# Storing a band of attention weights with shifted rows, and padding the next layer's weights earlier, in a two-layer kernel

## The chip, the core and the metric

The kernel runs on one core of a Trainium2 chip. Such a core has five engines with a queue of instructions each: TensorE (PE in the profile; its weight loads are shown apart as PEld), VectorE (DVE), ScalarE (ACT), GpSimd (POOL) and SyncE (SP), which here only issues transfers. Each queue runs in its order, and an instruction whose operands are not ready holds up everything behind it in its queue. Transfers between the core's memory and HBM are carried out by 16 DMA engines. The metric is the device time of one launch in microseconds (us); lower is better.

## The reference, cut to what matters

The input x has 4 rows (B) of 512 positions (T) with 128 channels (C). Two layers follow one another; each normalises x and adds an attention and a mixture of experts to it.

```python
# layer 0, attention: 16 heads, every position t sees the 64 positions that end with it
strain  = disp_win - disp[:, :, :, None, :]                  # 16 numbers per pair (t, d)
logits  = gelu(strain @ W_strain + rel_emb @ W_pos) @ W_bond \
          - 10 * sigmoid(gelu(strain @ W_dmg + b_dmg) @ W_dmg_out + b_dmg_out)
weights = softmax(where(in_range, logits, -inf))             # over the 64 distances
out     = einsum('bntd,bntde->bnte', weights, val_win)       # then @ W_cproj
# layer 0, experts: 16 gated experts, the best 4 of each position weigh in
# layer 1, attention: 16 heads of 8 channels over all 512 positions
q, k, v = split(x @ w_qkv)
out     = softmax(q k^T / sqrt(128)) v                       # then @ w_out
# layer 1, experts: 8 experts relu(x W1) W2, the best 2 of each position weigh in
```

So in layer 0 the attention weights of a row form a band: for every head and position, 64 numbers, one per distance.

## The kernel before

**Order of the program.** The kernel is written as generators, one for each job, which `weave` runs in turn by given step counts. The text's order gives each instruction its rank. A planner then places the instructions on the five queues: of those whose operands and buffers its estimated times say are ready, the one of the highest rank goes first. It also gives out the buffers of each pool and sets the semaphore waits. Every DMA takes one of a fixed set of completion semaphores, in turn. Where the planner's order was not wanted, explicit dependencies were added (`add_manual_dep`), as for the products of `hidden` (L378), which follow the products of layer 1's attention once these have begun.

**The rows' slots.** The loop at L719 goes over the rows b = 0 to 3. A slot weaves, for its own row, `band_logits(b)` and `gated_experts(b)`; for the row before, `band_values(b - 1)` and then the beginning of layer 1's `relu_experts(b - 1)`; for the row before that, the rest of `relu_experts`; and for the next row `prepare(b + 1)`. Each slot has two halves, two calls of `weave`. Layer 1's attention for all rows (`full_attention`) begins after the loop, woven with `band_values(3)` and what is left of the experts.

**band_logits (L543).** The 128 partitions hold 16 heads by 8 distances d8: partition 64 dq + 4 h + dd is head h at distance d8 = 4 dq + dd, and an outer loop `do` steps the distance by 8. For each `do` and each of the two kinds of activation, VectorE writes four differences into tiles z (L560, 128 x up to 2,048 numbers), ScalarE applies Gelu (L562, L566), and TensorE reduces them into a bank (L574). The pool of the z tiles has four buffers. At the end the maxima are exchanged over transposes (L603 to L612), and for each of two halves of `do` VectorE subtracts the maximum into a tile e, which is taken from the same four buffers (L616), ScalarE takes the exponential (L620), and one DMA stores e to a scratch tensor `by_t` in HBM (L621): 128 rows of 8 KB.

**band_values (L304).** For each of the row's four tiles of 128 positions (st), eight DMAs (L312) load a tile f from `by_t`: 128 partitions by 8 by 128 numbers. A weight belongs to the query position; to stand by the position it looks at, the row of distance d8 = 4 dq + dd is read from d8 places further on, which is why every (dq, dd) has its own DMA of 16 rows. `by_t` has rows of 8 T = 4,096 numbers (L291), and a last row of zeros for reads past the end (L476). TensorE transposes f (L321), ScalarE copies the result to g (L322), and g goes to a second scratch tensor `by_s` (L327), from which the tile wb is read back with a slanted pattern (L338) and multiplied with the values (L348, L352). f has two buffers.

**The weights of layer 1's attention.** After the loop and after layer 0's pools are closed, at L747 to L758: w_qkv is loaded (L748), a tile wqk is zeroed by GpSimd (L753), and VectorE copies the query and the key part into it, each head's 8 columns padded to 32 (L755). `queries` (L810) and `keys` (L819) multiply with wqk, `values` (L798) with w_qkv. Scores are products at L920, their maxima are taken by VectorE at L936.

**prepare (L492)** normalises row b and makes the projections from it, in three tiles of a pool `prep`: xn, xnT and sq, of 2 KB a partition each. The pool belongs to layer 0 and is closed with it; after `prepare(3)`, in row 2's slot, it is not used.

Of the kernel before, what the change touches and what calls it, by code (L numbers as in the profile page):

```python
# [22 lines left out]
FP = mybir.dt.float32  # L23
# [5 lines left out]
P = 128  # L29
# [3 lines left out]
H = 16  # L33
# [58 lines left out]
def weave(*tracks):  # L92
    for _ in woven(*tracks):
        pass
# [3 lines left out]
def two_layers(ctx: ExitStack, tc: tile.TileContext, w: dict, consts: bass.AP, out: bass.AP):  # L98
# [185 lines left out]

    chain = ctx.enter_context(tc.tile_pool(name="chain", bufs=2))
    wp = ctx.enter_context(tc.tile_pool(name="wp", bufs=2))
    xT = keep.tile([C, B * T], FP, name="xT")

    ROW = 8 * T  # L291
    by_t = dram.tile([P + 1, ROW], FP, name="by_t")
    by_s = dram.tile([T, H * BW], FP, name="by_s")

    wT_all = dram.tile([E0, P, 3 * P], FP, name="wT_all")
# [8 lines left out]
    def band_values(b, valn):  # L304

        o = chain.tile([P, TPB, C], FP, tag="o", name="o", bufs=1)
        for st in range(TPB):
            f = wp.tile([P, 8, P], FP, tag="f", name="f")
            for dq in range(2):
                for dd in range(4):  # L310
                    at = by_t.offset + (dq * 64 + dd) * ROW + st * P + 4 * dq + dd
                    nc.sync.dma_start(  # L312
                        out=f[dq * 64 + dd:(dq + 1) * 64:4],
                        in_=bass.AP(by_t.tensor, at, [[4 * ROW, H], [T + 8, 8], [1, P]]),
                    )
            yield
            g = wp.tile([P, H, WIN], FP, tag="g", name="g", bufs=1)
            for half in range(2):
                pt = bank()
                for i in range(4):  # L320
                    nc.tensor.transpose(pt[:, i * P:(i + 1) * P], f[:, 4 * half + i, :], ident)  # L321
                nc.scalar.copy(  # L322
                    g[:, :, 32 * half:32 * half + 32].rearrange("p h (q d) -> p q h d", d=4),
                    pt.rearrange("p (q h d) -> p q h d", h=H, d=4),
                )
            rows = by_s[st * P:(st + 1) * P, :]
            nc.sync.dma_start(out=rows.rearrange("s (h c) -> s h c", h=H)[:, :, 0:WIN], in_=g)  # L327
            v = va[st % 2]
            nc.scalar.copy(v[:, :, 0:8], valn[:, st, :].rearrange("p (h e) -> p h e", e=8))
            yield  # L330
            acc = bank()
            for half in range(2):
                wb = wp.tile([P, 8, BW], FP, tag="w", name="wb")
                for own in (True, False)[:1 + (st > 0)]:
                    s = st if own else st - 1
                    n = P if own else BW - P
                    at = by_s.offset + s * P * H * BW + half * 8 * BW + (0 if own else P)
                    nc.sync.dma_start(  # L338
                        out=wb[:, :, 0:P] if own else wb[:, :, P:BW],
                        in_=bass.AP(by_s.tensor, at, [[H * BW - 1, P], [BW, 8], [1, n]]),  # L340
                    )
                for g4 in range(2 * half, 2 * half + 2):
                    for own in (True, False)[:1 + (st > 0)]:
                        for hh in range(4):
                            h = g4 * 4 + hh
                            at = acc[hh * 32:hh * 32 + 32, g4 * P:(g4 + 1) * P]
                            if own:
                                nc.tensor.matmul(  # L348
                                    at, va[st % 2][:, h, :], wb[:, h % 8, 0:P], start=True, stop=(st == 0)
                                )  # L350
                            else:
                                nc.tensor.matmul(  # L352
                                    at[:, 0:BW - P], va[(st - 1) % 2][:, h, :], wb[:, h % 8, P:BW],
                                    start=False, stop=True,
                                )
            avs = chain.tile([P, 4, P], FP, tag="avs", name="avs", bufs=1)
            nc.scalar.copy(avs.rearrange("p g t -> p (g t)"), acc)
            pt = transposed(avs)
            pt3 = pt.rearrange("p (h e) -> p h e", h=H)
            rd = small.tile([P, H, 1], FP, tag="rd0", name="rd")  # L360
            nc.vector.reciprocal(rd, pt3[:, :, 8:9])
            nc.vector.tensor_tensor(
                o[:, st, :].rearrange("p (h e) -> p h e", h=H), pt3[:, :, 0:8],
                rd.to_broadcast([P, H, 8]), ALU.mult,
            )
            yield
# [89 lines left out]


    with ExitStack() as l0:
        prep = l0.enter_context(tc.tile_pool(name="prep", bufs=1))
        hold = l0.enter_context(tc.tile_pool(name="hold0", bufs=2))  # L460
        zp = l0.enter_context(tc.tile_pool(name="zp", bufs=4))
        lp = l0.enter_context(tc.tile_pool(name="lp", bufs=1))
# [10 lines left out]
        for st in range(TPB):  # L473
            nc.gpsimd.dma_start(out=by_s[st * P:(st + 1) * P, 0:2048], in_=zero)
            nc.gpsimd.dma_start(out=by_s[st * P:(st + 1) * P, 2048:H * BW], in_=zero[:, 0:H * BW - 2048])
        nc.gpsimd.dma_start(out=by_t[P:P + 1, 0:128], in_=zero[0:1, 0:128])  # L476


# [64 lines left out]
        def band_logits(b):  # L543
# [70 lines left out]
            for half in range(2):  # L614
# [3 lines left out]
                    pt[:, None, :].to_broadcast([P, 4, T]), ALU.subtract,  # L618
                )
                nc.scalar.activation(e, e, AF.Exp)  # L620
                nc.sync.dma_start(  # L621
                    out=by_t[0:P, 4 * half * T:(4 * half + 4) * T], in_=e.rearrange("p a t -> p (a t)")
                )
            yield

        def expert_weights(e, b):
# [20 lines left out]
        def gated_experts(b):  # L647
# [40 lines left out]
            finish(*late)  # L688
            add_rows(b, ya)

        preparation = prepare(0)
        for _ in range(2):
            next(preparation)
# [25 lines left out]
        for b in range(B):  # L719
            logits_b, gated_b = band_logits(b), gated_experts(b)  # L720
            if not b:
                weave((logits_b, 6), (preparation, 4))
            first = [(logits_b, 30 if b else 24), (gated_b, 7)]
            second = [(logits_b, 37), (gated_b, 10)]
            if b:
# [18 lines left out]
    def abank():  # L744
        return ps_a.tile([P, T], FP, tag="a", name="abank")

    w_qkv = one.tile([C, 3 * C], FP, name="w_qkv")  # L747
    nc.sync.dma_start(out=w_qkv, in_=w["L1_attn_w_qkv"])  # L748
    w_out = one.tile([C, C], FP, name="w_out")
    nc.sync.dma_start(out=w_out, in_=w["L1_attn_w_out"])  # L750

    wqk = one.tile([C, 2, 4, 4, 32], FP, name="wqk")
    nc.gpsimd.memset(wqk, 0.0)  # L753
    for s in range(2):
        nc.vector.tensor_copy(  # L755
            wqk[:, s, :, :, 0:8].rearrange("c g h e -> c (g h) e"),
            w_qkv[:, s * C:(s + 1) * C].rearrange("c (h e) -> c h e", e=8),
        )  # L758

    vaug = [one.tile([P, TPB, H, 32], FP, name=f"vaug{i}") for i in range(2)]  # L760
    nmax = [one.tile([P, TPB, 4, 32], FP, name=f"nmax{i}") for i in range(2)]
# [7 lines left out]
    def full_attention():  # L769
# [37 lines left out]
        def queries(n):  # L807
            b, g = groups[n]
            pq = abank()
            nc.tensor.matmul(  # L810
                pq, wqk[:, 0, g].rearrange("c h e -> c (h e)"), xT[:, b * T:(b + 1) * T], start=True, stop=True
            )
            q[n] = work.tile([P, T], FP, tag="q", name="q")
            nc.scalar.copy(q[n], pq)

        def keys(n):
            b, g = groups[n]
            pk = abank()
            nc.tensor.matmul(  # L819
                pk, wqk[:, 1, g].rearrange("c h e -> c (h e)"), xT[:, b * T:(b + 1) * T], start=True, stop=True  # L820
            )
            k[n] = work.tile([P, T], FP, tag="k", name="k", bufs=3)
            nc.scalar.activation(k[n], pk, AF.Identity, bias=c_("ones8"))
# [165 lines left out]
```

## Time and profile before

| | us |
|---|---|
| median of three runs | 1378.02 (1374.11 to 1379.18) |
| the profiled execution, its own time | 1381.3 |
| its span, first to last instruction | 1379.5 |
| TensorE busy | 1174.3 (85%) |
| VectorE busy | 1012.4 (73%) |
| ScalarE busy | 1018.5 (74%) |
| GpSimd busy | 96.9 (7%) |
| layer 0 | 0 to about 930 |
| the four pairs of stores by_t<-e issued from | 236.0, 470.8, 705.1, 929.6 |
| first product of layer 1's attention (L810) | 943.0 |

A busy time is the sum over the span; an engine at 85% on average can be full in one stage and half idle in another. The profile's chain of waits goes back from the last instruction, at each step to what released it. Its shares by engine are TensorE 59%, ScalarE 17%, VectorE 13%, DMA 6%. The time of a DMA is given from its issue on a queue to its landing. A queue's issue is an instruction of its own with its own length.

| DMA | times | KB each | us to landing | issue on SP, ns (least/median/most) |
|---|---|---|---|---|
| f<-by_t (L312) | 128 | 64 | 3.1 | 537/599/1790 |
| by_t<-e (L621) | 8 | 1,024 | | 319/320/320 |
| wb<-by_s (L338), the larger form | 32 | 512 | 4.1 | 360/527/2791, both forms |
| by_s<-g (L327) | 16 | 512 | 4.2 | 553/559/570 |
| wT<-wT_all (L630) | 48 | 192 | 3.0 | 319/320/1648 |
| r<-route (L672, L432) | 96 | 256 | 3.5 | 319/327/1532 (L672) |

### The profile page before, as it was taken

Reading aid. Unit: us, or ns where it says so; the run is one execution under the profiler, and the core shown is the slowest. Engines: PE = TensorE matmul, PEld = TensorE weight load, DVE = VectorE, ACT = ScalarE, POOL = GpSimd, SP = SyncE. Lnnn points to the kernel's source line nnn. Section 1 sums busy time; section 2 is a strip of 40 time slices with the busy share of each in tenths; the row PEclk is TensorE's granted clock in tenths of the full one; section 3 lists DMA queues with packets and bytes.
Section 4 is the critical chain, followed back from the end, with each engine's and each line's share of the span. In section 5 each row is a group of like instructions: output and inputs, shape, how many; then the busy total and the mean of one; then the engine's idle time right before and its main releaser. Section 6 shows DMA issues by size and latency. Waiting matters only on the chain.

```text
span 1379.5 us, 17426 instructions
## 1 busy us (share of the span) xinstructions
PE 1174.3 (85%) x6763; PEld 450.2 (33%) x6763; DVE 1012.4 (73%) x1085; ACT 1018.5 (74%) x1160; POOL 96.9 (7%) x68
## 2 busy tenths in 40 slices
PE   5676976678889789889989988887999899999997
PEld 2122323123433323353333334232333332333322
DVE  4999998999866999987799998843444434444451
ACT  4899997999968899988889988862454435545554
POOL 2000000000000002200002320012000000000000
PEclk9799998899879999999999999999999989999999
DMA  7121213446212445622244751235133200011100
GB/s 268 44 74 52 76 52 103 100 118 153 62 41 75 150 102 145 170 64 64 73 153 110 180 131 48 67 96 166 49 88 77 69 9 24 24 38 39 31 16 8
DMA packets 168524, 117.61 MB, mean 85 GB/s; under 512 B 66621, under 2 KB 149274, under 8 KB 166906
## 3 DMA queue, kind: packets, MB, share of 16 engines
q1 hardware_dynamic: 166970, 109.77, 29.3%
q0 software_dynamic: 1184, 6.29, 1.2%
q8 instruction: 54, 0.88, 0.3%
q10 hardware_dynamic: 288, 0.43, 0.1%
q14 instruction: 28, 0.23, 0.1%
HBM read 89.00 MB, written 27.46 MB: 84 GB/s over the span
## 4 chain that ended last, share of the span: by engine, by line
PE 59%; ACT 17%; DVE 13%; DMA 6%; issue 5%; SPq 0%; DVEq 0%; ACTq 0%
PE score L920 11%; PE lbank L574 10%; PE bank L381 8%; PE bank L442 7%; ACT z L566 6%; DVE z L560 5%; PE accbank L838 4%; ACT z L562 3%; PE gbank L674 3%; PE accbank L663 3%; DMA wb<-by_s 3%; PE gbank L681 2%; DMA wT<-wT_all 2%; DVE nmax L936 2%; PE abank L810 1%
## 5 line engine op out<-in xcount | busy, mean ns | idle before, releaser
L560 DVE TENSOR_TENSOR z<-proj 128x2044 f32<-128x2044 f32 (+31 forms) x256 | 554.1, 2189 | 29.0 <-PE lbank L574 12.6
L574 PE MATMUL lbank<-z,place 128*32 128x504 f32 (+18 forms) x2048 | 288.9, 639 | 110.1 <-ACT z L566 68.8
L936 DVE TENSOR_REDUCE nmax<-score 128x2 f32<-128x1024 f32 x128 | 156.3, 1225 | 182.3 <-PE score L920 180.1
L566 ACT ACTIVATE z<-z,posb 128x1024 f32<-128x1024 f32 (+31 forms) x256 | 267.3, 1097 | 10.2 <-DVE z L560 8.2
L942 ACT ACTIVATE ex<-score 128x1024 f32<-128x1024 f32 x128 | 130.3, 1023 | 159.7 <-PE score L920 159.7
L562 ACT ACTIVATE z<-z,brep 128x2048 f32<-128x2048 f32 (+31 forms) x128 | 241.4, 1906 | 5.3 <-DVE z L560 4.9
L920 PE MATMUL score<-k,q 32*128 32x512 f32 x512 | 152.2, 655 | 13.9 <-DVE nmax L936 11.7
L447 POOL TENSOR_TENSOR total<-total,part 128x512 f32<-128x512 f32 x32 | 82.6, 2580 | 1038.3 <-DVE part L446 1038.3
L920 PE MATMUL score<-qa,k 32*128 32x512 f32 x512 | 139.7, 648 | 2.1 <-ACT ex L942 2.1
L381 PE MATMUL bank<-xT,ew 128*128 128x512 f32 x256 | 136.2, 626 | 1.6 <-ACT h L389 0.8
L442 PE MATMUL bank<-h,ew 128*128 128x512 f32 x256 | 133.1, 619 | 4.7 <-issue 4.7
L389 ACT ACTIVATE h<-bank,cols 128x512 f32<-128x512 f32 x144 | 97.1, 684 | 45.3 <-PE bank L381 44.6
L574 PEld LDWEIGHTS lbank<-z,place 128*32 128x32 f32 x2048 | 43.0, 112 | 264.2 <-ACT z L566 143.9
L663 PEld LDWEIGHTS accbank<-wT,lin 128*128 128x128 f32 x512 | 72.2, 204 | 60.4 <-issue 34.6
L663 PE MATMUL accbank<-wT,lin 128*128 128x128 f32 x512 | 82.1, 297 | 10.1 <-DVE lin L661 10.1
L674 PE MATMUL gbank<-tT,wT 128*128 128x512 f32 x128 | 72.2, 647 | 17.4 <-DMA wT<-wT_all 16.5
L838 PE MATMUL accbank<-ex,vaug 128*32 128x512 f32 x512 | 70.8, 619 | 0.2 <-ACT ex L942 0.2
L681 PE MATMUL gbank<-tT,wT 128*128 128x512 f32 x128 | 70.6, 635 | 0.0
L920 PEld LDWEIGHTS score<-k,q 32*128 32x128 f32 x512 | 41.2, 187 | 89.0 <-ACT ex L942 44.1
L442 PEld LDWEIGHTS bank<-h,ew 128*128 128x128 f32 x256 | 44.2, 193 | 74.4 <-issue 71.0
L381 PEld LDWEIGHTS bank<-xT,ew 128*128 128x128 f32 x256 | 41.9, 192 | 72.8 <-issue 43.6
L659 DVE SCALAR_TENSOR_TENSOR lin<-lin,r 128x512 f32<-128x512 f32 x64 | 44.5, 695 | 28.6 <-ACT lin L683 28.3
(188 smaller groups left out, 1193.7 us busy)
## 6 DMA issues: line engine op xcount, KB each, us to landing
r<-route SPq DMA_DIRECT2D x96, 256.0 KB, 3.5
ew<-in_L_ffn_W SPq DMA_DIRECT2D x64, 256.0 KB, 3.4
wb<-by_s SPq DMA_DIRECT2D x32, 512.0 KB, 4.1
wT<-wT_all SPq DMA_DIRECT2D x48, 192.0 KB, 3.0
by_t<-e SPq DMA_DIRECT2D x8, 1024.0 KB
f<-by_t SPq DMA_DIRECT2D x128, 64.0 KB, 3.1
by_s<-g SPq DMA_DIRECT2D x16, 512.0 KB, 4.2
wb<-by_s SPq DMA_DIRECT2D x24, 256.0 KB, 3.6
```

Of the source, the lines that this page charges most:

```text
L381: mm = nc.tensor.matmul(ph, wt[:, c * P:(c + 1) * P], xT[:, b * T:(b + 1) * T], start=True, stop=True)
L442: nc.tensor.matmul(py, old[1][:, c, :], old[0][c], start=(c == 0), stop=(c == 3))
L560: nc.vector.tensor_tensor(z[:, :, :, 0:n], seen, own, ALU.subtract)
L562: nc.scalar.activation(z[:, :, :, 0:n], z[:, :, :, 0:n], AF.Gelu, bias=b_dmg)
L566: last = nc.scalar.activation(z[:, dq, :, 0:n], z[:, dq, :, 0:n], AF.Gelu, bias=posb[:, j:j + 1])
L574: mm = nc.tensor.matmul(ps[q:q + 32, t0:T], place[:, kind, 3 - dd:35 - dd], z[:, dq, hg, 0:n], start=(dd == 0), stop=(dd == 3),)
L663: nc.tensor.matmul(ya[:, i * P:(i + 1) * P], lin[:, i * P:(i + 1) * P], wT[:, 2, :], start=False, stop=(e == E0 - 1 and i == TPB - 1),)
L674: nc.tensor.matmul(pg, wT[:, 0, :], tT, start=True, stop=True)
L838: mm = nc.tensor.matmul(av[n][r:r + 32, :], vaug[b % 2][:, i, g * 4 + h, :], ex[n, i][:, h, :], start=(i == 0), stop=(i == TPB - 1),)
L920: mm = nc.tensor.matmul(ps[:, h - two, :], own[r, i * P:(i + 1) * P], seen[r, :], start=True, stop=True)
L936: freed.append(nc.vector.tensor_reduce(nmax[n % 2][:, i, two:two + 2, 8:9], ps, AX.X, ALU.max, negate=True))
L942: freed.append(nc.scalar.activation(ex[n, i][:, two:two + 2, :], ps, AF.Exp, scale=inv))
```

## The change

The rows of `by_t` get 8 more numbers (PITCH = 8 T + 8), and each row is stored d8 = 4 dq + dd places earlier than before. The store of a half is now eight DMAs of 16 rows, one for each (dq, dd), instead of one of 128 rows; the load of a tile f is one DMA of 128 rows, instead of eight of 16. Because the shifted rows leave up to 8 numbers unwritten between one row and the next, GpSimd zeroes 24 numbers around each row's end once at the start. The pool `prep` is opened with the outer pools and stays open. The padding of layer 1's weights becomes a function `attention_weights`, called at the head of row 3's slot: it takes three tiles from `prep` under the tags of `prepare`'s tiles, sq for w_qkv, xn and xnT for the padded query and key weights (two tiles in place of one wqk, zeroed one by one).

```diff
     wp = ctx.enter_context(tc.tile_pool(name="wp", bufs=2))
+    prep = ctx.enter_context(tc.tile_pool(name="prep", bufs=1))
...
-    ROW = 8 * T
-    by_t = dram.tile([P + 1, ROW], FP, name="by_t")
+    PITCH = 8 * T + 8
+    by_t = dram.tile([P + 1, PITCH], FP, name="by_t")
...
             f = wp.tile([P, 8, P], FP, tag="f", name="f")
-            for dq in range(2):
-                for dd in range(4):
-                    at = by_t.offset + (dq * 64 + dd) * ROW + st * P + 4 * dq + dd
-                    nc.sync.dma_start(
-                        out=f[dq * 64 + dd:(dq + 1) * 64:4],
-                        in_=bass.AP(by_t.tensor, at, [[4 * ROW, H], [T + 8, 8], [1, P]]),
-                    )
+            nc.sync.dma_start(
+                out=f, in_=bass.AP(by_t.tensor, by_t.offset + st * P, [[PITCH, P], [T + 8, 8], [1, P]])
+            )
...
-        prep = l0.enter_context(tc.tile_pool(name="prep", bufs=1))
...
+        nc.gpsimd.dma_start(
+            out=bass.AP(by_t.tensor, by_t.offset + PITCH - 16, [[PITCH, P], [1, 24]]), in_=zero[:, 0:24]
+        )
         nc.gpsimd.dma_start(out=by_t[P:P + 1, 0:128], in_=zero[0:1, 0:128])
...
                 nc.scalar.activation(e, e, AF.Exp)
-                nc.sync.dma_start(
-                    out=by_t[0:P, 4 * half * T:(4 * half + 4) * T], in_=e.rearrange("p a t -> p (a t)")
-                )
+                for dq in range(2):
+                    for dd in range(4):
+                        at = by_t.offset + (dq * 64 + dd) * PITCH - 4 * dq - dd + 4 * half * T
+                        nc.sync.dma_start(
+                            out=bass.AP(by_t.tensor, at, [[4 * PITCH, H], [1, 4 * T]]),
+                            in_=e[dq * 64 + dd:(dq + 1) * 64:4].rearrange("h a t -> h (a t)"),
+                        )
...
+        def attention_weights():
+            w_qkv = prep.tile([C, 4, C], FP, tag="sq", name="w_qkv").rearrange("c a e -> c (a e)")
+            nc.sync.dma_start(out=w_qkv[:, 0:3 * C], in_=w["L1_attn_w_qkv"])
+            wqk = [prep.tile([C, 4, 4, 32], FP, tag=t, name="wqk") for t in ("xn", "xnT")]
+            for s in range(2):
+                nc.gpsimd.memset(wqk[s], 0.0)
+                nc.vector.tensor_copy(
+                    wqk[s][:, :, :, 0:8].rearrange("c g h e -> c (g h) e"),
+                    w_qkv[:, s * C:(s + 1) * C].rearrange("c (h e) -> c h e", e=8),
+                )
+            return w_qkv, wqk
...
             logits_b, gated_b = band_logits(b), gated_experts(b)
             if not b:
                 weave((logits_b, 6), (preparation, 4))
+            if b == B - 1:
+                w_qkv, wqk = attention_weights()
...
-    w_qkv = one.tile([C, 3 * C], FP, name="w_qkv")
-    nc.sync.dma_start(out=w_qkv, in_=w["L1_attn_w_qkv"])
     w_out = one.tile([C, C], FP, name="w_out")
     nc.sync.dma_start(out=w_out, in_=w["L1_attn_w_out"])
-
-    wqk = one.tile([C, 2, 4, 4, 32], FP, name="wqk")
-    nc.gpsimd.memset(wqk, 0.0)
-    for s in range(2):
-        nc.vector.tensor_copy(
-            wqk[:, s, :, :, 0:8].rearrange("c g h e -> c (g h) e"),
-            w_qkv[:, s * C:(s + 1) * C].rearrange("c (h e) -> c h e", e=8),
-        )
```

In `queries` and `keys`, `wqk[:, 0, g]` and `wqk[:, 1, g]` become `wqk[0][:, g]` and `wqk[1][:, g]`.

More of the change, by code (lines that the diff above doesn't have):

```diff
@@ L810, in queries @@
             nc.tensor.matmul(
-                pq, wqk[:, 0, g].rearrange("c h e -> c (h e)"), xT[:, b * T:(b + 1) * T], start=True, stop=True
+                pq, wqk[0][:, g].rearrange("c h e -> c (h e)"), xT[:, b * T:(b + 1) * T], start=True, stop=True
             )
@@ L819, in keys @@
             nc.tensor.matmul(
-                pk, wqk[:, 1, g].rearrange("c h e -> c (h e)"), xT[:, b * T:(b + 1) * T], start=True, stop=True
+                pk, wqk[1][:, g].rearrange("c h e -> c (h e)"), xT[:, b * T:(b + 1) * T], start=True, stop=True
             )
```

## The prediction

> **What bounds the kernel now.** I read the table of busy time by stretch first, then what the loaded tile f waits for and who waits for it, then the timelines of SP, VectorE and TensorE around the four stores and around the change of layer. The columns of the first view are: stretch, its length, busy us (and instructions) of TensorE, its weight loads, VectorE, ScalarE and GpSimd, then granted clock, DMA share and GB/s.
>
> ```profile
> 240.00:330.00 90.00, 65.56 (x538) 22.46 (x538) 88.70 (x65) 85.92 (x83) 0.00 (x0) 0.91 0.51 125
> 640.00:705.00 65.00, 60.73 (x268) 25.65 (x267) 50.09 (x55) 53.65 (x68) 4.19 (x3) 0.97 0.25 77
> 1160.00:1380.00 220.00, 208.44 (x1132) 67.12 (x1132) 97.12 (x106) 110.26 (x130) 10.18 (x8) 0.98 0.08 25
> ```
>
> See three regimes. In the first half of a row's slot in layer 0 VectorE is busy 88.70 of 90 us, ScalarE 85.92: an idle microsecond of VectorE there is a lost one. In the second half TensorE leads (60.73 of 65). In layer 1 TensorE is busy 95% to the end, so only a start that comes earlier, or a TensorE gap that closes, moves the end. DMA is half idle everywhere: bytes are not the limit, waits are.
>
> **Part 1, loads: eight become one.** The view of tile f (duration ns min/median/max, first and last start):
>
> ```profile
> L312 SPq DMA_DIRECT2D f<-by_t x128: 537/599/1790, 243.1 to 1014.1; - x128
> L321 PEld LDWEIGHTS bank<-cst,f x128: 137/141/230, 258.5 to 1078.2; 128*128 128x128 f32 x128
> DMA to landing us min/median/max: 2.3/3.1/5.4
> ```
>
> A tile's eight issues cost SP 8 x (0.60 + 0.04 between two) = 5.1 us. One issue of the same 1,024 pieces is that of wb<-by_s of 512 KB: 0.37 to 0.58 us, landing 4.1 us later by the page's sixth part. So 4.5 us of SP go per tile, 16 x 4.5 = 72 us in all. What is that worth? Pairing the 128 issues by eights with the transposes of L321, the last issue of a tile comes 8.9 to 64.4 us before its first transpose, and lands after at most 5.4: at least 3.5 us of cover for each of the 16 tiles. The trace shows no TensorE transpose waiting for f. Here a rule of the Trainium skill can be weighed (DMA: Bandwidth & Descriptors, Rules for kernel authors): "Coalesce into one large transfer; under 64 KB you're paying mostly overhead". f's pieces are just 64 KB. With that page's fixed 2.0 us paid in series, 7 x 2.0 x 16 = 224 us would go, as an estimate. The row says 72 us, of SP's time, behind other work. I take **0**. What could be late next on SP? After the loads come wb, wT and r; but wb waits for the landing of by_s<-g (4.2 us), wT for L663, so they are not released by a freer SP. If the cover were gone, a tile would win 4.5 us less the longer landing (4.1 against 2.3), 2.7 us.
>
> **Part 1, stores: two become sixteen a row.** This is where the change can lose. SP and VectorE at the end of row 0:
>
> ```profile
> 236.03 2.12 SPq L621 DMA_DIRECT2D by_t<-e  x2
> 238.25 0.61 SPq L672 DMA_DIRECT2D r<-route  x1
> 243.15 7.04 SPq L312 DMA_DIRECT2D f<-by_t  x11
> ```
> ```profile
> 238.33 0.69 DVE L661 SCALAR_TENSOR_TENSOR lin<-glu,lin 128x512 f32<-128x512 f32 x1
> 240.03 13.41 DVE L560 TENSOR_TENSOR z<-proj 128x2040 f32<-128x2040 f32 x6 [1.01 <-DMA by_t<-e]
> ```
>
> The tiles e lie in two of the four buffers z, and the third subtraction of the next row waits (1.01 us idle) until the first store has landed, at 240.0, 4.0 us after its issue. In rows 1 and 2 the same place has no slack either: stores at 470.78 and 705.05, VectorE's next subtraction at 474.82 and 709.05, released by the store within 0.2 us of VectorE being free. So the landing of the first half is on the path of the engine that bounds this stage.
>
> After: eight DMAs of 16 rows of 8 KB, 128 KB each. No row shows this shape; the nearest are the 16-row loads at the start:
>
> ```profile
> 1.79 0.41 SPq L135 DMA_DIRECT2D bonds<-in_L_attn_W_dmg  x1
> 2.25 0.42 SPq L136 DMA_DIRECT2D bonds<-in_L_attn_W_bond  x1
> 2.71 0.42 SPq L137 DMA_DIRECT2D bonds<-in_L_attn_W_dmg_out  x1
> ```
>
> One every 0.46 us. Bounds: 0.36 (a store with an idle queue before it took 0.32, plus 0.04) and 0.64 (f's). I take **0.46**, the row with as many pieces. Landing of the last: 1.9 us (wT_all<-wT, 192 KB, the page's sixth part). Then e's first half lands 7 x 0.46 + 1.9 = 5.1 us after the first issue, against 4.0, 4.1 and 4.1 when VectorE needs it: +1.1, +1.0, +1.0 = **+3.1 us**. Ends: 0.36 gives 4.4, +1.0 in all; 0.64 gives 6.4, +7.0 in all. The second half lands at 15 x 0.46 + 1.9 = 8.8; its buffer is wanted 8.55, 9.5 and 9.5 us after the first issue, shifted by the 1.1 already counted: no further wait, but +0.5 in row 0 at 0.64. Row 3 has no next subtraction.
>
> The page's other rule speaks against this edit: of two transfers to disjoint partition halves it says "Don't bother", they share the same engines, use one of 128 partitions. By it the split brings nothing and only the issues count, as here; its neighbour, that issue time is "usually small relative to the DMA itself" (Issuing engines are not separate DMA queues), would make the sum 0. The rows say 3.2 us of issue beside a landing of 1.9, so I keep 3.1. That the rows now begin off a round address cannot be priced: loads that do so (f, wb) have the same 27 ns a piece as the round ones, no store does it.
>
> What stands behind the stores on SP: w2 (L430), r (L432) and wT (L630) in rows 1 and 2. SP is free 16 x 0.46 = 7.4 us after the first issue instead of 2.1. wT went at 476.37 and landed 4.9 us later, with a 1.29 us wait of TensorE; now it goes at about 479.4, beside stores that are nearly through, and lands in some 3 us: 482.4, +1.1, which is the shift that VectorE has anyway. Row 2 works out at 716.7 against 714.6, +2.1, 1.0 beyond the shift; TensorE idles 0.79, 1.58 and 1.01 us for z just after, which takes it. I take 0, ends 0 and +2. The first f goes after the last landing, near +9 us instead of +7.1, and lands at about +13: its transposes stand at +22.
>
> That sixteen stores wait for one another, being rows that interleave, is answered by the zeroing of by_s, whose rows interleave too: GpSimd issues at 4.28, 4.98, 5.51, 6.03 without a wait, though each takes 9.4 us to land. The new zeroing of the gaps is one more such issue, 0.5 us on GpSimd, idle from 10.5 to 215.9; even if the next one waits for it, nobody waits for them before 236. Cost 0, with the pitch of 8 more columns.
>
> **Part 2, the weights.** Today the change of layer reads, on TensorE:
>
> ```profile
> 938.45 3.60 PE L442 MATMUL bank<-h,ew 128*128 128x512 f32 x8
> 943.02 1.12 PE L810 MATMUL abank<-xT,wqk 128*128 128x512 f32 x2 [0.97 <-DVE wqk L755]
> 944.82 1.12 PE L819 MATMUL abank<-xT,wqk 128*128 128x512 f32 x2 [0.68 <-ACT q L814]
> 946.72 1.14 PE L920 MATMUL score<-k,q 32*128 32x512 f32 x8 [0.78 <-ACT k L823]
> 947.79 1.16 PE L798 MATMUL abank<-w_qkv,xT 128*128 128x128 f32 x8
> 950.38 1.14 PE L920 MATMUL score<-k,q 32*128 32x512 f32 x8 [1.43 <-DVE nmax L936]
> ```
>
> SP issues w_qkv at 938.10 (1.34 us), the copies of L755 run at 942.75, the first query product follows. With the weights ready, queries and keys can go between the expert products of 924 to 942, and three gaps close: 0.97 + 0.68 + 0.78 = **-2.4 us**. The next gaps (1.43, 1.38, 1.97, 2.09, up to 966.70) wait for VectorE's maxima at 2.37 us a pair; they close only if the maxima themselves start beside expert products. Ends: 0, if the products keep their order, and -9.3, if all go. The two copies move into a stage where VectorE is full: 2 x 0.22 = **+0.4**. The zeroing (0.96 on GpSimd) and one load of 192 KB move to where GpSimd and DMA have room; nobody waits for them: 0.
>
> **Sum**: 0 + 3.1 + 0 - 2.4 + 0.4 = +1.1 us. The profiled execution took 1381.3 us (span 1379.5, 1.8 around it), so 1382.4 there; the median of the three runs is 1378.0, so **1379 us**.
>
> **Rivals.**
> - *The stores hold the buffers longer* (slower): pitch 0.64, place L560 after each store: +7.5, wT +2.0, copies +0.4, nothing gained at the layer: +9.9, 1388 us. For it: e's buffer has no slack, f's row is the longest record of such issues. Against: sixteen pieces, not 128. It decides from a cost of the stores of 6.5 us (without the gain at the layer), a pitch of about 0.6.
> - *The layers overlap* (faster): the maxima start beside the last expert products, all gaps close: -9.3 + 1.0 + 0.4 = -7.9, 1370 us. For it: TensorE has 8 us of expert products from 934.58 on that attention could fill around. Against: layer 1's buffers lie where e lay and come free only when the later store lands, near 938.4.
> - *The stores are chained after all* (the edit does not give what it says): the first half lands after 8 x 1.9 = 15.2, the second after 30.4; per row 11.1 and then about 10.5 of waiting, three rows, +65: 1443 us. Against: the by_s row.
>
> **How the numbers follow.** No change 0.45, stores 0.34, overlap 0.16, chained 0.05. A measurement tells 0.5%, 6.9 us, from no change. Slower 0.39 (stores and chain), faster 0.15 (nearly all of the overlap), same 0.46. The likeliest case's own range is 1372 to 1385; the range over the cases goes from 1367 to 1396, beyond 1388 since an order of work shifted by the new times would add to the stores' loss.
>
> **What would show it.** Right: L560's third subtraction of rows 1 to 3 idle 1 to 2 us longer, released by by_t<-e; sixteen store issues 0.46 apart; f's transposes unmoved against their neighbours; the first L810 before 943, with no wait on L755. Wrong: issues 0.6 or more apart, transposes or wb that come earlier and close a TensorE gap, or a gap of layer 1 (wb at 1087.58, 4.34 us) that changes.

## The result, and the profile after

| | before | after |
|---|---|---|
| median, us | 1377.67 (6 runs) | 1446.94 (1437.43 to 1450.21, 6 runs) |
| ratio, 95% interval | | 1.050 [1.046, 1.053] |
| span of the profiled run | 1379.5 | 1447.2 |
| TensorE busy, us | 1174.3 | 1207.3 |
| mean granted clock of TensorE | 0.941 | 0.91 |
| row slots, from one row's first store to the next's | 234.7, 234.3, 224.6 | 248.9, 256.7, 246.5 |
| after the last row's first store | 449.9 | 457.9 |

The kernel became slower by 69 us, far outside the range. The loss comes in every slot in which a row's band is turned and multiplied: 14.2, 22.4, 21.9 and 8.0 us. The first slot has no such work and lost 1.2.

First the part that the prediction thought dangerous: the stores. The tile view of `by_t` after the change (line, queue, operation, count, issue in ns least/median/most, first and last start):

```profile
L623 SPq DMA_DIRECT2D by_t<-e x64: 472/587/599, 237.3 to 998.8; - x64
L310 SPq DMA_DIRECT2D f<-by_t x16: 359/371/972, 260.0 to 1064.5; - x16
```

The timeline of SP after, beginning at the first row's stores (start, us, what, how many):

```profile
237.25 9.99 SPq L623 DMA_DIRECT2D by_t<-e  x16
247.35 0.53 SPq L633 DMA_DIRECT2D wT<-wT_all  x1
247.97 0.40 SPq L675 DMA_DIRECT2D r<-route  x1
259.49 0.32 SPq L633 DMA_DIRECT2D wT<-wT_all  x1
260.00 0.99 SPq L310 DMA_DIRECT2D f<-by_t  x2
```

Sixteen issues take 9.99 us, one every 0.63, where two took 2.12. Each lands 2.3 us after its issue (the median), and none waits for another. VectorE's timeline at the place the prediction watched:

```profile
240.33 0.69 DVE L664 SCALAR_TENSOR_TENSOR lin<-glu,lin 128x512 f32<-128x512 f32 x1
244.47 4.47 DVE L559 TENSOR_TENSOR z<-proj 128x2040 f32<-128x2040 f32 x2 [3.45 <-PE lbank L573]
```

The third subtraction is later (244.47 against 240.03), but by this view TensorE releases it, not the store. The reason stands in the two programs: it no longer takes a buffer of e. These are the buffers, A to D, of row 1's first 24 tiles z; row 0's two tiles e lay in A and D:

```
before      C B A C D B A C D B A C D B A C D B A C D B A C
after       C B C B C B C B C B D C B D C B D C B D C A B D
```

Before, the third tile takes A and the fifth D. After, ten tiles alternate between two buffers, so each has to wait for the products of the tile two places before it; D comes back with the 11th and A with the 22nd, 31.9 and 58.5 us after the first store, though the last store has landed after some 12. VectorE's busy time in the 50 us from the first stores of rows 0, 1 and 2, added up, before and then after (length, then busy us by engine, then means):

```profile
sum 150.00, PE 117.10 PEld 37.69 DVE 147.56 ACT 144.95 POOL 14.02; mean PE 39.03 PEld 12.56 DVE 49.19 ACT 48.32 POOL 4.67
sum 150.00, PE 94.28 PEld 19.95 DVE 127.72 ACT 122.08 POOL 3.31; mean PE 31.43 PEld 6.65 DVE 42.57 ACT 40.69 POOL 1.10
```

VectorE, which bounds this stage, loses 20 of 150 us. Now look at the tile f. Before, it was transposed at 258.46. After, its load is issued at 260.00 and lands some 5 us later, yet TensorE's timeline reads:

```profile
265.13 1.06 PE L573 MATMUL lbank<-z,place 128*32 128x509 f32 x8 [1.95 <-ACT z L565]
267.62 1.91 PE L573 MATMUL lbank<-z,place 128*32 128x504 f32 x8 [1.44 <-ACT z L561]
271.23 1.91 PE L573 MATMUL lbank<-z,place 128*32 128x503 f32 x8 [1.70 <-ACT z L561]
...
279.62 3.88 PE L573 MATMUL lbank<-z,place 128*32 128x504 f32 x16 [1.82 <-ACT z L565]
...
299.62 1.04 PE L318 MATMUL bank<-cst,f 128*128 128x128 f32 x8
```

TensorE idles again and again between 265 and 294 for ScalarE's z, while f lies ready: the transposes stand behind these products **in its queue**. The order of the queue has changed too. Where the first transposes of the four tiles stand can be counted in groups of eight products of `lbank` (64 groups to a row; row 1 begins at 64), from the two programs:

```
            row 1            row 2              row 3
before      72 80 89  98    136 144 154 164    200 208 218 228
after       84 90 98 106    148 156 164 172    212 220 228 236
```

Each row's band work begins 12 groups later, a fifth of a row. What does it delay? In the second half of the slot, the experts of the row before. The group in which VectorE takes the experts' products (last column: idle time before it, and what ended it), before and then after:

```profile
L446 DVE TENSOR_TENSOR part<-bank,r 128x512 f32<-128x512 f32 x32 | 22.0, 686 | 29.2 <-PE bank L442 22.5 <-issue 5.5 <-DMA r<-route 1.1
```
```profile
L443 DVE TENSOR_TENSOR part<-bank,r 128x512 f32<-128x512 f32 x32 | 22.0, 687 | 75.4 <-PE bank L439 64.0 <-DMA by_t<-e 6.7 <-issue 4.6
```

46 us more of VectorE's time is idle here. Most of it lies at the end of the slots, as VectorE's timeline shows:

```profile
447.04 0.69 DVE L443 TENSOR_TENSOR part<-bank,r 128x512 f32<-128x512 f32 x1 [11.57 <-PE bank L439]
...
454.27 0.69 DVE L443 TENSOR_TENSOR part<-bank,r 128x512 f32<-128x512 f32 x1 [6.54 <-PE bank L439]
```

So the first half of a slot, in which VectorE and ScalarE bound, lost the TensorE work that could run beside them; that work stood in the second half, where TensorE bounds, and VectorE waited for it. This wait and the one for buffers at the slot's beginning are two things, and the experiments part them.

### The profile page after: what moved, and what is told of

Read it like the earlier page. It is cut to its first block, busy times and chain, and to the rows that moved or that the text cites. A ratio compares the mean times of both kernels' runs of the same rounds, so it can differ in the third digit from the quotient of the medians.

```text
span 1447.2 us, 17384 instructions
## 1 busy us (share of the span) xinstructions
PE 1207.3 (83%) x6763; PEld 449.1 (31%) x6763; DVE 1014.6 (70%) x1085; ACT 1023.5 (71%) x1159; POOL 57.9 (4%) x70
## 4 chain that ended last, share of the span: by engine, by line
PE 53%; ACT 17%; DVE 13%; DMA 11%; issue 5%; SPq 0%; POOL 0%; DVEq 0%; POOLq 0%; ACTq 0%
PE score L929 10%; PE lbank L573 9%; PE bank L378 8%; DVE z L559 6%; ACT z L565 6%; PE bank L439 5%; ACT z L561 4%; DMA wb<-by_s 4%; PE accbank L847 4%; DMA by_s<-g 3%; PE gbank L677 3%; PE accbank L666 3%; DMA wT<-wT_all 2%; DVE nmax L945 2%; PE gbank L684 2%
## 5 line engine op out<-in xcount | busy, mean ns | idle before, releaser
L559 DVE TENSOR_TENSOR z<-proj 128x2044 f32<-128x2044 f32 (+31 forms) x256 | 557.2, 2192 | 36.3 <-PE lbank L573 22.4
L573 PE MATMUL lbank<-z,place 128*32 128x504 f32 (+18 forms) x2048 | 313.7, 689 | 126.5 <-ACT z L565 65.6
L929 PE MATMUL score<-k,q 32*128 32x512 f32 x512 | 156.4, 680 | 13.1 <-DVE nmax L945 11.1
L439 PE MATMUL bank<-h,ew 128*128 128x512 f32 x256 | 129.7, 608 | 4.3 <-issue 4.3
L666 PE MATMUL accbank<-wT,lin 128*128 128x128 f32 x512 | 85.1, 303 | 17.5 <-DVE lin L664 17.5
L677 PE MATMUL gbank<-tT,wT 128*128 128x512 f32 x128 | 74.7, 667 | 22.8 <-DMA wT<-wT_all 22.1
L444 POOL TENSOR_TENSOR total<-total,part 128x512 f32<-128x512 f32 x32 | 43.0, 1345 | 1086.3 <-DVE part L443 1086.3
L443 DVE TENSOR_TENSOR part<-bank,r 128x512 f32<-128x512 f32 x32 | 22.0, 687 | 75.4 <-PE bank L439 64.0
(190 smaller groups left out, 1207.3 us busy)
```

Of the source, the lines that this page charges most:

```text
L439: nc.tensor.matmul(py, old[1][:, c, :], old[0][c], start=(c == 0), stop=(c == 3))
L559: nc.vector.tensor_tensor(z[:, :, :, 0:n], seen, own, ALU.subtract)
L573: mm = nc.tensor.matmul(ps[q:q + 32, t0:T], place[:, kind, 3 - dd:35 - dd], z[:, dq, hg, 0:n], start=(dd == 0), stop=(dd == 3),)
L666: nc.tensor.matmul(ya[:, i * P:(i + 1) * P], lin[:, i * P:(i + 1) * P], wT[:, 2, :], start=False, stop=(e == E0 - 1 and i == TPB - 1),)
L677: nc.tensor.matmul(pg, wT[:, 0, :], tT, start=True, stop=True)
L929: mm = nc.tensor.matmul(ps[:, h - two, :], own[r, i * P:(i + 1) * P], seen[r, :], start=True, stop=True)
```

## The experiments

Three theories stood at the start. A: the planner's order of the band's work sets the time. B: the sixteen stores' own time does, as in the prediction. C is that the moved weights (part 2) cost or gain. All ratios are against runs of the kernel before on the same chip (medians 1376.6 to 1378.6).

**Part 2 alone.** The diff's lines for `prep` and `attention_weights`, nothing of the band:

```diff
+            if b == B - 1:
+                w_qkv, wqk = attention_weights()
```

> Part 2 alone: stores and loads of the band as before, the weights padded at the head of row 3's slot. If the loss lies in the place of the band's work (theory A: the planner takes the 16-row stores to land late and puts each tile's transposes about 12 groups of products later on TensorE) or in the stores' own time (theory B), this kernel stays within 6 us of before: 1372 to 1384, with the 2.4 us of the change of layer won and up to 6 us lost where VectorE's copies wait in its queue for w_qkv. If the weights are what costs (theory C), it is slower by 15 us or more.

1371.98 us, ratio 0.997 [0.996, 0.998]: -4.7 us. Part 2 is a small gain and does not make the loss.

**The stores by rows alone.** The tensor keeps its pitch, a half's store is split, the loads stay eight:

```diff
+                for dq in range(2):
+                    for dd in range(4):
+                        at = by_t.offset + (dq * 64 + dd) * ROW + 4 * half * T
...
+                            out=bass.AP(by_t.tensor, at, [[4 * ROW, H], [1, 4 * T]]),
```

> The split of the stores alone, without shift and with the eight loads of before; it computes the same. The planner's order puts the first tile's transposes after 16 groups of row 1 instead of 8, later even than in the changed kernel (12). Theory A: the whole loss or more, 1435 to 1460. Theory B: the stores' own cost alone, three rows of at most 2.5 us on VectorE and 2 on wT: 1380 to 1392. Theory C: as before, 1378.

1464.68 us, 1.064 [1.061, 1.066]. The split by itself makes more than the whole loss, and a little more than theory A asked for. The transposes now stand at 88, 97, 107, 116.

**The same number of stores, by columns.** As many DMAs and bytes, on the same queue, but each of 128 rows by 256 numbers:

```diff
+                for c in range(8):
+                    nc.sync.dma_start(
+                        out=by_t[0:P, 4 * half * T + c * 256:4 * half * T + c * 256 + 256],
...
```

> Sixteen stores a row as in the split kernel, the same bytes and the same count of issues, but each of 128 rows by 1 KB instead of 16 rows by 8 KB. The planner leaves the transposes where they were (after 9 groups instead of 8). Theory A: near before, 1376 to 1392, though SP issues as long and the buffers of e come free as late. Theory B: as slow as the split by rows, whatever that turns out to be.

1388.62 us, 1.009 [1.006, 1.013]: +12.0 us. The transposes stand at 73, 81, 90, 99, one group from before, and e's buffers come back almost as before, with row 1's third and sixth tile z. The view of `by_t`, SP's timeline, and the three stretches of 50 us:

```profile
L622 SPq DMA_DIRECT2D by_t<-e x64: 319/447/455, 233.3 to 935.4; - x64
```
```profile
233.31 7.68 SPq L622 DMA_DIRECT2D by_t<-e  x16
241.09 0.39 SPq L674 DMA_DIRECT2D r<-route  x1
```
```profile
sum 150.00, PE 115.00 PEld 34.39 DVE 146.99 ACT 143.02 POOL 19.45; mean PE 38.33 PEld 11.46 DVE 49.00 ACT 47.67 POOL 6.48
```

These sixteen issues hold SP 7.68 us against 9.99, and land after 1.9 us against 2.3. That is little beside the 76 us between the two kernels, whose orders differ by 15 groups; VectorE, at 146.99, loses nothing at the slots' beginnings. Why only a split by rows moves the order and the buffers is an inference about the planner, drawn from the programs alone: it seems to price a DMA by what one partition moves, so that a store of 16 rows of 8 KB counts as much as one of 128 rows, and eight of them as eight full stores, while a store of 1 KB a row counts an eighth. By its estimate f and e's buffers then come late, and it puts other work and other buffers first.

**The single load alone.** One DMA per tile from an unshifted tensor. This leaves out the shift between distances, so weights of neighbouring distances stand beside the values.

```diff
+            nc.sync.dma_start(
+                out=f, in_=bass.AP(by_t.tensor, by_t.offset + st * P, [[ROW, P], [T + 8, 8], [1, P]])
+            )
```

> The single load alone, from unshifted rows with the store of before; the band is left unshifted, so the weights are those of other distances, at the same cost. The planner puts the transposes 3 to 9 groups earlier. Theory A: a small gain or none, 1365 to 1380, since the order moves the other way and f was covered by at least 3.5 us. Theory B: no change, 1378.

1361.96 us, 0.991 [0.988, 0.993]: -14.7 us, a larger gain than either theory asked for. The transposes move forward to 67, 74, 82, 90. By the same inference, eight loads of 16 rows had been priced too high before; one is not.

**Only the order.** Before's transfers, all of them. Empty steps move a tile's transposes, and what follows from them, later in the text's order, with the count of steps in `weave` raised to match; a dependency also holds each tile's first transpose behind a product of the next row:

```diff
+            if b < B - 1:
+                for _ in range(60 if not st else 3):
+                    yield
...
+                    if b < B - 1 and not half and not i:
+                        tc.add_manual_dep(
+                            turn.ins, summed[b + 1][AT[st]].ins.name,
...
-                first.append((band_values(b - 1, ready[b - 1][1]), 14))
+                first.append((band_values(b - 1, ready[b - 1][1]), 83))
```

> The transfers, tiles and weights of before, unchanged; only the order differs: dependencies hold each tile's transposes back behind a product of row b, so that they stand after 20, 27, 35 and 43 groups of the row, as in the changed kernel (20, 26, 34, 42), instead of 8, 16, 25 and 34. Theory A (order alone): 1425 to 1455, most of the 69 us. Theory B (the stores' time): 1378, or at most 1390.

1411.13 us, 1.025 [1.021, 1.028]: +33.8 us, with no transfer changed in form or number; less than theory A asked for, more than B. The transposes stand at 84, 92, 100, 108, within two groups of the change, and row 1's tiles z have the buffers that they had before. The group of the experts' products, and the three stretches of 50 us:

```profile
L456 DVE TENSOR_TENSOR part<-bank,r 128x512 f32<-128x512 f32 x32 | 22.0, 686 | 75.2 <-PE bank L452 61.7 <-DMA w_out<-in_L_attn_w_out 6.7 <-issue 5.6
```
```profile
sum 150.00, PE 125.26 PEld 35.10 DVE 146.54 ACT 142.68 POOL 36.89; mean PE 41.75 PEld 11.70 DVE 48.85 ACT 47.56 POOL 12.30
```

75.2 us idle, as in the changed kernel (75.4), from the order alone; and almost nothing lost at the slots' beginnings (146.54).

**The change with the order put back.** The whole change, plus dependencies by which the products wait in the queue behind a tile's transposes, at the old places or a little before them (72, 80, 88, 94 in row 1):

```diff
+    AT = [8, 16, 25, 34]
...
+                                    if tied and not dq and not hg and 8 * do + 4 * (1 - kind) + dd >= AT[tied[0][0]]:
+                                        tc.add_manual_dep(mm.ins, tied.pop(0)[1].ins.name, ...)
```

> The changed kernel with its sixteen stores and its single load, and with dependencies that put the transposes back to the places they had before (after 8, 16, 24 and 30 groups of row 1, 8, 16, 25 and 34 of rows 2 and 3). Theory A: the loss goes, 1372 to 1395; what is left above before is the stores' own cost, about 10 us by the split into columns, less what the weights (5 us) and the load give. Theory B: it stays above 1430.

1403.58 us, 1.020 [1.016, 1.024]. That is 43.4 us less than the change, and 26.2 more than before: between what theories A and B asked for. The same group, the three stretches, and the group of the subtractions:

```profile
L447 DVE TENSOR_TENSOR part<-bank,r 128x512 f32<-128x512 f32 x32 | 22.0, 689 | 29.8 <-PE bank L443 21.2 <-issue 8.4
```
```profile
sum 150.00, PE 103.21 PEld 32.18 DVE 123.86 ACT 120.83 POOL 3.31; mean PE 34.40 PEld 10.73 DVE 41.28 ACT 40.28 POOL 1.10
```
```profile
L563 DVE TENSOR_TENSOR z<-proj 128x2044 f32<-128x2044 f32 (+31 forms) x256 | 556.8, 2193 | 47.2 <-PE lbank L577 31.9 <-ACT z L569 7.0 <-ACT proj L509 6.0
```

29.8 us, as before (29.2): the wait goes with the order. The wait for buffers stays. Row 1's first ten tiles z again alternate between two buffers, VectorE is busy 123.86 of the 150 us, and it idles 47.2 us before the subtractions (29.0 before the change), 31.9 of it for products of `lbank` (12.6).

**Fewer stores with the shift kept.** If A holds, the change's idea can be had without the sixteen stores. Each half goes as two DMAs of 64 rows with a slanted pattern, with part 2 and without:

```diff
+                    at = by_t.offset + dq * (64 * PITCH - 4) + 4 * half * T
...
+                        out=bass.AP(by_t.tensor, at, [[4 * PITCH, H], [PITCH - 1, 4], [1, 4 * T]]),
```

> The whole change, with the shifted store of a half as two DMAs of 64 rows (one for each dq, the shift of dd in the pitch) instead of eight of 16. The planner puts the transposes after 5, 12, 19 and 25 groups of row 1, earlier than before. Theory A: at the level of the single load alone or below it, 1353 to 1370. Theory B: between before and the split into columns, 1376 to 1388, since four issues a row cost little.

> The same stores and load without part 2. The difference to the kernel with the weights moved says whether part 2 adds its 5 us beside the earlier order: theory A 1358 to 1373, some 3 to 6 us above the kernel with both.

1372.63 us, 0.998 [0.996, 0.999], and 1381.6 us, 1.003 [1.001, 1.004]; theory A had asked for less than 1370 and 1373. The order was as early as with the single load (69, 76, 83, 89), but of its 14.7 us nothing is to be seen. The view of waits of the two-store kernel with part 2, SP's queue (who waits for what, us in total, times, longest):

```profile
SPq L622 <- DMA by_t<-e: 20.0, 8, 3.3
```

Here the stores do wait for one another: the ranges of addresses of a row's two halves overlap when the pattern is slanted, though their elements do not. TensorE's tile view shows no wait for f here, so how this took the gain away is not shown.

**One slanted store per half.** The store carries only the shift by dd, which one pattern can say for all 128 rows; the load, two DMAs of 64 rows, carries that by dq.

```diff
+                at = by_t.offset + dq * (64 * PITCH + 4) + st * P
...
+                    out=bass.AP(by_t.tensor, at, [[4 * PITCH, 2 * H], [PITCH - 1, 4], [1, 4 * T]]),
```

> The whole change with the shift divided between store and load: the store lays down only the part of the shift that depends on the row modulo 4 and stays one DMA of 128 rows per half; a tile is loaded by two DMAs of 64 rows, one for each half of the partitions. The transposes of f stand at groups 68, 76, 83, 89 of the products of rows 1 to 3's places (before 72, 80, 89, 98). Theory A (the order of the band's work sets the time): the earlier order brings what the single load alone brought, 12 to 15 us, and the weights some 4 more: 1356 to 1364 us, ratio 0.985 to 0.99. Theory B (the stores' own time sets it): no store is split, so nothing is lost there and nothing won by the order: what the weights alone gave, 1372 us. Pairs of 64-row stores that waited for one another cost the two-store form its gain: if so, the stores here are issued no more than 2.5 us apart and the time lies under 1368.

> The same as the run before it without part 2 (the weights stay in layer 1). Theory A: 1361 to 1368 us, as with the single load alone, ratio about 0.99. Theory B: as before, 1376 to 1379. Theory C (the weights are worth 4 to 9 us in any order): the kernel with part 2 is faster than this one by that much.

1373.14 us, 0.997 [0.995, 0.998], and 1379.47 us, 1.001 [0.999, 1.002]. Theory A had asked for 1356 to 1364 and missed: an order as early as that of the single load was worth nothing here. SP and TensorE of the kernel without part 2 show a part of why:

```profile
235.65 0.59 SPq L624 DMA_DIRECT2D by_t<-e  x1
238.07 0.33 SPq L676 DMA_DIRECT2D r<-route  x1
240.80 0.52 SPq L624 DMA_DIRECT2D by_t<-e  x1
246.07 2.65 SPq L311 DMA_DIRECT2D f<-by_t  x4
```
```profile
252.18 1.30 PE L320 MATMUL bank<-cst,f 128*128 128x128 f32 x5 [3.42 <-DMA f<-by_t]
```

The second store goes 5.15 us after the first (1.8 before), f is issued at 246.07, and TensorE now idles for it: its products 6.2 us in three places by the tile view, against 0.3 with the single load alone. (Its weight loads wait 8.9 and 3.1 us over the same stretches; the 15 us in the next expectation add the two up, and so count twice.) That suggests that an early place in the queue is a gain only if the data is there, which the next form tries.

**Two tensors.** Each half gets a tensor of its own with a pitch of 4 T + 8. A half goes as two slanted stores of 64 rows, whose ranges do not meet; a tile is loaded by two DMAs of 128 rows, one from each tensor:

```diff
+    PITCH = 4 * T + 8
+    by_t = [dram.tile([P + 1, PITCH], FP, name=f"by_t{i}") for i in range(2)]
...
+            for half in range(2):
+                at = by_t[half].offset + 32 * half + st * P
...
+                    in_=bass.AP(by_t[half].tensor, at, [[PITCH, P], [T + 8, 4], [1, P]]),
```

> The whole change with the band's weights in two tensors, one for each half of e: a half is stored by two slanted DMAs of 64 rows whose address ranges do not meet, a tile is loaded by two DMAs, one from each tensor. Transposes of f at groups 68, 76, 83, 89 and 132, 141, 149, 157 of the products, as with the single load alone. Theory A2 (an earlier order is worth something only if the data is there: in the one-store form the second store waited 4.5 us for the first to land, f came later, and TensorE waited 15 us for f): the stores here are issued under 2 us apart within a half and without a wait between halves, TensorE waits under 6 us for f, and the time is 1357 to 1366 us, ratio 0.985 to 0.992. Theory D (the shift itself, rows off a round address or more descriptors, costs the difference): 1370 to 1374, as in the two forms before.

> The run before without part 2. Theory A2: 1361 to 1370 us, as the single load alone (1362) or a little over. Theory D: 1378 to 1382. Theory C: 4 to 9 us slower than the run with part 2.

**1363.05 us, 0.990 [0.988, 0.992]**, and 1371.72 us, 0.996 [0.994, 0.998] without part 2. SP's timeline of the first:

```profile
235.37 5.04 SPq L626 DMA_DIRECT2D by_t<-e  x4
241.97 1.78 SPq L312 DMA_DIRECT2D f<-by_t  x2
```

f goes 6.6 us after the first store, against 10.4 with one slanted store; no store waits for another, and TensorE's tile view shows no wait for f. With nearly the same order of the transposes as with one slanted store, the two kernels are 10 and 8 us faster. The whole form is faster than before and after by more than measurement blurs (13.8 us under before). Without part 2 it is some 2 us above what was expected and 9.8 above the single load, so this form is not free either; what those 9.8 us are was not tried.

**Part 1 alone, with the change's order and with the old.** Open was whether part 2 loses inside the change, as VectorE waits 6 us there for w_qkv. The first kernel is the change without the lines of `attention_weights`, the second adds the dependencies that put the order back:

```diff
-            if b == B - 1:
-                w_qkv, wqk = attention_weights()
```

> Part 1 of the change alone, as the change has it (sixteen stores a row, one load a tile, the shift and its gap), with the weights left in layer 1. If part 2 is worth its 5 to 9 us here too (theory C): 1452 to 1456 us. If its wait for the load of w_qkv, 6.0 us of VectorE in the changed kernel, eats that: 1443 to 1449.

> Part 1 alone with the transposes tied to their old places. If the wait for w_qkv (6.8 us of VectorE in the same kernel with part 2) is a cost that this order brought on: 1396 to 1402, faster than the 1403.6 of the kernel with part 2 or equal to it. If what is left over before's time comes from the stores and from the other loads behind them (rows 2 and 3 some 17 and 8 us longer), not from part 2: 1407 to 1413.

1451.12 us, 1.052 [1.049, 1.055], and 1406.56 us, 1.020 [1.018, 1.022], each just outside the ranges expected. Putting the transposes back is worth 44.6 us without part 2, 43.4 with it. Each kernel taken against its own runs of before, part 2 is worth some 3 and 2 us in these orders, within the spread of the runs: less than the 6 to 9 in the last three pairs, and no loss that a measurement shows.

**The account.** Of the 69 us, 34 to 45 are the order of the transposes, shown both ways. Part 1 with that order put back still takes 28 us more; sixteen stores by columns take 12 more. The other 16 no run isolates. The likeliest source is the buffers of e, held back in every kernel that stores 16 rows at a time: with the order put back VectorE is busy 24 us less at the slots' beginnings than before, by columns or with the order alone only 1 us less. A part of these 24 us is made up later in the slots, so they can't simply be added to the order's share. No kernel gave the buffers back and left the rest; the wT, r and expert loads that the planner placed anew behind the stores are not separated from it, nor is VectorE's idle time of 7.3 us before the copy of w_qkv, where part 2 is in.

## Why the prediction was wrong

**The step that failed** is the one that costs the stores by their issues and landings in an order taken as fixed: "The first f goes after the last landing, near +9 us instead of +7.1, and lands at about +13: its transposes stand at +22." f went at +22.7, behind wT, and landed some 5 us later, but the transposes stood at +62: some 35 us after the data was there. In its place the runs show the order: moved alone it costs 33.8 us, put back it gives 43.4. The buffers were taken as fixed in the same way: the +3.1 us of the stores are the wait of a third subtraction for e's first half, a wait that the change does not have. The front part says that a planner orders the queues and gives out the buffers by estimated times; the prediction priced how long the stores take on the chip and never asked what the planner would believe of them. It left "an order of work shifted by the new times" to half a sentence that widened the range to 1396.

**Pitch of the stores.** 0.46 was taken, by the count of pieces, and 0.63 measured; the upper end 0.64 was right. f's row, eight loads of 16 rows, was the nearer one. It moved little: the place that should have waited, the third subtraction after a store, is released by TensorE and no longer uses e's buffer. By columns, where e's buffers are used almost as the prediction took them, sixteen stores at 0.48 cost 12.0 us, not some 3; only 1.9 us of that show at the subtractions as waits for `by_t<-e`.

**Loads, 0.** Right that the eight issues were hidden: TensorE waits for f in neither kernel. Wrong as a price: the single load alone gave 14.7 us. An earlier order came with it; whether SP's freed time has a part in the gain, no run separates. The text named this under what would prove it wrong, "transposes or wb that come earlier and close a TensorE gap", and priced it nowhere.

**Weights, -2.4 + 0.4.** Measured -4.7 alone; the direction was right, the size too small. The change's layer boundary on TensorE shows which gaps went:

```profile
996.50 3.60 PE L439 MATMUL bank<-h,ew 128*128 128x512 f32 x8
1002.76 1.38 PE L828 MATMUL abank<-xT,wqk 128*128 128x512 f32 x2 [2.67 <-ACT q L823]
1004.92 2.09 PE L929 MATMUL score<-k,q 32*128 32x512 f32 x8 [0.78 <-ACT k L832]
```

The wait on the copy is gone. Those for ScalarE's q and k stand, the first longer than before (0.68): the three gaps did not all close. Not foreseen was the wait of the copy itself, moved among VectorE's work:

```profile
L702 DVE COPY wqk<-w_qkv 128x128 f32<-128x128 f32 x2 | 0.5, 248 | 6.0 <-DMA w_qkv<-in_L_attn_w_qkv 6.0
```

**wT, 0.** The products that wait for wT idle 22.1 us for it against 16.5: 5.6 more, above the end of 2; how much of it reaches the end was not measured.

**The zeroing, 0.** Right: the DMA behind it on GpSimd, that of the last row, waits 14.8 us and goes near 24; nobody waits for it.

**The rivals.** "Chained" named 1443, near the result, but by luck, for another reason: the sixteen stores go 0.63 apart, and SP shows no wait of one store for another. Chained stores did appear in the forms with slanted rows, which the argument from the zeroing of by_s did not cover. No rival was a shift of the order or of the buffers.

## What to carry to other kernels

Where a planner orders the queues, a DMA has two prices: what it takes on the chip, and what the planner thinks. Here stores that held SP for 10 us moved work by a fifth of a row and kept two of four buffers back for 30 to 60 us. So compare the order of the instructions and the buffers of the tiles, before and after an edit, ahead of pricing the waits, and ask of each new DMA shape how it is estimated. Work that fills TensorE's gaps in a stage bound by another engine is lost when it slips into the stage that TensorE bounds; a place earlier in the queue need not pay if its data does not come as early.

## What the runs showed of the hardware

**Issue time follows the shape, not the bytes.** On SP one store of 1 MB in 128 rows took 0.32 us to issue, one of 128 KB in 16 rows 0.59 (median), one of 128 KB in 128 rows of 1 KB 0.45.

**The granted clock was lower where TensorE's work became thin.** Three windows of the first half of row 1's slot, of before, of the order alone, and of the change. The columns are stretch, length, busy us (and instructions) of TensorE, its loads, VectorE, ScalarE, GpSimd, then granted clock, DMA share and GB/s:

```profile
258.00:300.00 42.00, 28.46 (x277) 10.00 (x269) 41.03 (x32) 38.74 (x35) 0.00 (x0) 0.92 0.58 136
```
```profile
258.00:300.00 42.00, 28.32 (x163) 7.55 (x166) 40.08 (x29) 37.33 (x35) 0.00 (x0) 0.85 0.15 40
```
```profile
262.00:296.00 34.00, 21.52 (x106) 2.91 (x106) 31.54 (x21) 26.99 (x20) 0.00 (x0) 0.66 0.13 36
```

The busy shares are close (68, 67, 63%), the clock is 0.92, 0.85 and 0.66: with busy time weighed by the clock, as an estimate from these rows, TensorE did 62, 57 and 42% of what it could. A product of `lbank` took 689 ns on average after, 639 before. That the thin work causes the lower clock, and so slows such a stage a second time, is the reading that these windows suggest; no run holds the one and changes the other. The kernel with the order put back does not follow it throughout: in the 50 us from the first stores of rows 0 and 1 TensorE was busy 30.06 and 37.45 us, at 0.82 and 0.76.
